# Two-level Strassen for left and right from block 2 on, and all second-level weight pieces in iteration 0

## Chip, cores and metric

The kernel runs on one core of a Trainium2 chip. The metric is device time in microseconds for the whole program, from one launch; the kernel before takes 2949.6 us (median of three runs, 2948.95 to 2950.2). All data is fp32. A core has five engines: PE (matrix products), DVE, ACT and POOL (elementwise work), and SP, which here only issues DMAs. ACT and POOL issue some DMAs too. Each engine takes its instructions in one order.

## What is computed

Two graph layers on 128 graphs of 64 nodes with 768 features. Only layer 0's products with W_left and W_right, and what lies around them in time, are touched by the change.

```python
# layer 0, per graph (h = x, 64 x 768; adjacency 64 x 64)
p = softmax(h @ h.T / sqrt(768)); delta = p * adjacency
attn = delta / (delta.sum(-1, keepdims=True) + 1e-10)
h_left, h_self, h_right = (h @ W.T + b for W, b in left, self, right)
ctx = upper(attn) @ h_left + diag(attn)[:, None] * h_self + lower(attn) @ h_right
x1 = layernorm(h + relu(layernorm(ctx) * gamma + beta))
# layer 1, 12 heads of 64
q, k, v = x1 @ Wq + bq, x1 @ Wk + bk, x1 @ Wv + bv
scores = where(adj > 0, q @ k.T / 8 + beta * adj, -9e15)
out = layernorm(x1 + concat_heads(softmax(scores) @ v))
```

## The kernel before

**Blocks and stages.** The 8192 rows are worked on as 16 blocks of 512 rows (8 graphs). A block needs six 512 x 768 x 768 products: left, right, self (layer 0), q, k and v (layer 1). Each is done by Strassen's algorithm, which replaces eight products of half-size matrices by seven: `seven` (L354) runs over `ORDER`, the seven products i, and over two halves j. That makes 14 *places*, numbered 0 to 13, each of three products on PE (recorded as six instructions, two passes each). A Strassen sum of activations is formed on POOL (`combined` L301, `combined4` L315), a Strassen piece of a weight was formed once at the program's start and is streamed from HBM by SP.

**Iteration n of the main loop** works on layer 0 of block m = n + 1 and layer 1 of block n, in this order: left and right of block m (`left` and `right`), self (`own`), v of block n (`val`, in which the context products of block m stand too, `context0` L647), then q and k in three groups of heads hg 0, 1, 2 (`qk[0]` to `qk[2]`, `projected` L776). Iteration 0 has only `val` and `qk`; block 1's layer 0 is done before the loop. The dictionaries in brackets are *hooks*: a function put at a place of such a stage is called in front of that place's products.

**One level and two.** For m below `DEEP` (3), left and right are two calls of `side_part` (L585), each a `seven`. From block 3 on they are one call of `both_sides` (L603): `nested` (L409) does Strassen's algorithm twice, 7 x 7 = 49 products of left and right side by side, in the outer order `ORDER2`. Its 49 steps are counted as 28 places, those of left (0 to 13) and then those of right (14 to 27). The sums of the second level are formed on POOL by `second_level` (L320), into a tile with two buffers (`s2_p`); the nine pieces of a weight product are loaded by SP as tiles `wlr` from `lr_d` (L617), 63 loads for a block.

**Where the second-level weight pieces come from.** `deepened(i)` (L243) has three parts. `begin` loads the four half-pieces of product i into tiles `w_deep` (4 DMAs on SP) and copies the plain parts in HBM (4 DMAs on POOL, L254 and L255); two calls of `formed` (L257, L260) do four subtractions each on DVE; `end` (L262, L266) stores four results with POOL's DMAs. The tiles come from the pool `wst`, 19 buffers that all streamed weights (`wl`, `wr`, `ws`, `wv`, `wqk`, `wlr`) share. The three parts after `begin` are put at the head of the queue `urgent` three places later.

**The order of the work around the products.** No scheduler moves the instructions of the loop: on each engine they stand in the order in which the Python code issues them. What DVE and ACT do beside the products (softmax, norms, transposes) is put with `later` (L121) in one of three queues, `first`, `urgent` and `lazy`. After each place, `step` (L135) takes at most one full DVE item from them, with an ACT item before it where one is at the head. `settle(key)` (L157) takes items until none of that key is left: whatever needs a result settles it first. In `nested`, `step` takes no lazy item at three of the seven products.

**Names that matter below.** `attention0` (L498) needs block m's transposed rows `hT` (`turned` L289, six DVE transposes at L294), computes `u` (L516) and queues its softmax. `scores` (L804) computes `sc` (L822) for one group of heads and queues its softmax (L826, L847 to L849 on DVE, 16 ACT exponentials L840, two DVE transposes L844); `weighted` (L853) multiplies the result with v (L869) and adds it on DVE (L875, L879). `uqk` (L791) is ACT's read of a q or k product, `q`, `k` (L799) DVE's. `finish_by_act` (L884) is the last layernorm of block p = n - 1: four row sums on ACT (L921), a scaling on DVE (L896), four sums of squares on ACT (L924), DVE (L899), a root on ACT, DVE (L905, L906), four ACT normalisations (L910) and the stores (L914). `stored` (L705) settles layer 0's result of block n and stores it to HBM as `x1d`; `squares` (L278) then loads it as `sq` by four DMAs on ACT's queue (L285), in rows of short pieces, for the transposes of layer 1. In iteration 1 `stored` is at place 1 of `right` and the four `sq` loads are at places 2 to 5 of `right`; in later iterations they are at place 4 and at places 10 to 13 of `left`.

Of the kernel before, what the change touches and what calls it, by code (L numbers as in the profile page):

```python
# [13 lines left out]
ALU = mybir.AluOpType  # L14
# [4 lines left out]
B, L, D = 128, 64, 768  # L19
# [3 lines left out]
HALF = D // 2  # L23
# [21 lines left out]

ORDER2 = (7, 1, 2, 6, 5, 4, 3)
MATRICES = (1, 2, 8, 3, 9, 5, 7, 4, 6)
DEEP = 3


@with_exitstack
def gnn_two_layers(ctx: ExitStack, tc, x, adj, wl, bl, ws, bs, wr, br, gamma, beta,
                   wq, bq, wk, bk, wv, bv, abeta, out):
    nc = tc.nc
# [35 lines left out]
    bias_lr = const.tile([P, 2, D], F32, tag="bias_lr", name="bias_lr")  # L90
# [66 lines left out]
    def settle(key):  # L157

        for queue in (first, urgent, lazy):
            while any(item[0] == key or item[0][0] == key for item in queue):  # L160
                queue.popleft()[1]()
# [81 lines left out]
    def deepened(i):  # L243


        w = {}

        def begin():
            for j, nm in enumerate("lr"):
                src = pieces[nm][i]  # L250
                for k in range(2):
                    w[j, k] = wst.tile([P, 2, QUAD], F32, tag="w", name="w_deep")
                    nc.sync.dma_start(out=w[j, k], in_=src[:, k, :].rearrange("p (h c) -> p h c", h=2))
                nc.gpsimd.dma_start(out=lr_d[i - 1, 0:3, :, j, :].rearrange("m p c -> p m c"), in_=src[:, :, 0:QUAD])  # L254
                nc.gpsimd.dma_start(out=lr_d[i - 1, 3:5, :, j, :].rearrange("m p c -> p m c"), in_=src[:, 1:3, QUAD:HALF])  # L255

        def formed(j):  # L257
            b11, b12, b21, b22 = (w[j, k][:, h, :] for k in range(2) for h in range(2))
            for out, a, b in ((b11, b12, b11), (b12, b22, b12), (b22, b22, b11), (b21, b21, b22)):
                nc.vector.tensor_tensor(out, a, b, ALU.subtract)  # L260

        def end():  # L262
            for j in range(2):
                for k in range(2):
                    d = lr_d[i - 1, 5 + 2 * k : 7 + 2 * k, :, j, :].rearrange("m p c -> p m c")
                    nc.gpsimd.dma_start(out=d, in_=w[j, k])  # L266

        return begin, [(partial(formed, 0),), (partial(formed, 1),), (end, "gap")]
# [9 lines left out]
    def squares(rows):  # L278


        sq = sq_p.tile([P, SQ, Q * KC], F32, tag="sq", name="sq")
        by_group = rows.rearrange("(s j) (a f) -> a j s f", j=Q, a=P // Q)

        def load(a):
            nc.scalar.dma_start(out=sq[a * Q : (a + 1) * Q], in_=by_group[a])  # L285

        return sq, [partial(load, a) for a in range(P // Q)]
# [13 lines left out]
    def combined(xT, n=None):  # L301
# [6 lines left out]
        S = {1: a11, 2: a12, 4: a22, 5: s1, 6: s2, 7: a21}  # L308
        if n is not None and n >= DEEP:

# [696 lines left out]
    for n in range(NBLK):  # L1007
        m, p = n + 1, n - 1
        left, right, own, val = {}, {}, {}, {}
        qk = [{}, {}, {}]  # L1010

        def at(hooks, place, f, *args):
            hooks.setdefault(place, []).append(partial(f, *args))

        def spread(hooks, place, fs):
            for k, f in enumerate(fs):
                at(hooks, place + k, f)


        for i, (when, hooks, place) in zip(ORDER2, ((0, val, 2), (0, val, 8), (0, qk[0], 8), (0, qk[1], 6),  # L1020
                                                    (0, qk[2], 6), (1, own, 3), (1, val, 3))):
            if when == n:
                begin, steps = deepened(i)
                at(hooks, place, begin)
                at(hooks, place + 3, lambda i=i, steps=steps: urgent.extendleft([(("d", i), *f) for f in reversed(steps)]))

        last = n == NBLK - 1
        if p >= 0:
            one = left if not last else qk[0]
            at(one, 2, scores, p, 2, *((1,) if last else (2, None, 4)))  # L1030
            at(one, 5, weighted, p, 1)
            if not last and m < DEEP:
                at(left, 13, weighted, p, 2)
                at(right, 0, finish_by_act, p)
            elif not last:
                at(right, 1, weighted, p, 2)
                at(right, 2, finish_by_act, p)
            else:
                at(qk[1], 5, weighted, p, 2)

        if not last:
            if n > 0:
                if m + 1 < NBLK:
                    at(left, 4, edges, m + 1)
                at(*((left, 11) if m < DEEP else (right, 13)), sides, m)
                sq1 = {}

                def begin1():
                    blocks[n]["sq1"], sq1["fs"] = squares(blocks[n]["x_d"])


                when, place = (left, 10) if n > 1 else (right, 2)
                at(when, place, begin1)
                fetch = {}

                def begin2():
                    fetch["fs"] = loads(m)

                at(right, 8, begin2)
                for t in range(T):  # L1060
                    at(right, 8 + t, lambda t=t: fetch["fs"][t]())
                for a in range(P // Q):
                    at(when, place + a, lambda a=a: sq1["fs"][a]())
                at(own, 0, settle, ("f", p))

                def turn1():
                    blocks[n]["xT"] = turned(("t1", n), blocks[n]["sq1"], f"xT_{n}")
                    later(("m", n), *mask(n), queue=urgent)

                at(own, 3, turn1)  # L1070

                def sums1():
                    settle(("t1", n))
                    blocks[n]["S"] = combined(blocks[n]["xT"])

                at(own, 11, sums1)
                at(val, 0, lambda: combined4(blocks[n]["S"]))
                at(left, 6, lambda: combined4(blocks[m]["S"]))
                at(*((left, 4) if n > 1 else (right, 1)), blocks[n]["stored"])
                if m + 1 < NBLK:  # L1080
                    sq = {}

                    def begin():
                        blocks[m + 1]["sq"], sq["fs"] = squares(x_b[m + 1])

                    at(own, 11, begin)
                    for a in range(P // Q):
                        at(own if a < 3 else val, 11 + a if a < 3 else 0, lambda a=a: sq["fs"][a]())
                if m == DEEP:
                    settle("d")  # L1090
                if m < DEEP:
                    side_part(m, "l", None, left)
                    side_part(m, "r", None, right)
                    at(own, 0, lambda: nc.vector.tensor_tensor(bias_lr[:, :, HALF:D], bias_lr[:, :, HALF:D],
                                                               bias_lr[:, :, 0:HALF], ALU.subtract))
                else:
                    for t, f in enumerate(both_sides(m, {**left, **{2 * len(ORDER) + k: f for k, f in right.items()}})):
                        at(own, 1 + t, f)
                self_part(m, None, own)
            tiles, normal = context0(m)  # L1100
            for t, f in enumerate(tiles):
                at(val, 1 + 2 * t, f)
            for hooks, place, f in ((val, 9, normal[0]), (val, 13, normal[1]), (qk[0], 1, normal[2])):
                at(hooks, place, f)
            if m + 1 < NBLK:

                def turn0():
                    blocks[m + 1]["hT"] = turned(("t", m + 1), blocks[m + 1]["sq"], f"hT_{m + 1}")

                at(val, 6, turn0)  # L1110

                def scores0():
                    settle(("t", m + 1))
                    attention0(m + 1, False)

                def sums0():
                    blocks[m + 1]["S"] = combined(blocks[m + 1]["hT"], m + 1)

                at(qk[0], 4, scores0)
                at(qk[2], 8, sums0)  # L1120

        if not last:
            values(n, val)
        else:
            transposed1(n)
            at(qk[0], 9, lambda: later(("m", n), *mask(n), queue=urgent))
            blocks[n]["S"] = combined(blocks[n]["xT"])
            combined4(blocks[n]["S"])
        at(qk[1], 2, scores, n, 0)
        at(qk[2], 2, scores, n, 1)  # L1130
        if not last:
            at(qk[2], 5, weighted, n, 0)
        for hg in range(NHG):
            projected(n, hg, qk[hg])
# [49 lines left out]
```

## Time and profile before

| | |
|---|---|
| median of the runs | 2949.6 us |
| the profiled execution | 2950.66 us, of which the span is 2949.0 |
| PE busy | 2881.7 us, 17578 matrix instructions |
| DVE, ACT, POOL busy | 1993.3, 1125.9, 731.1 us |
| iteration 0 (block 0's layer 1), 212.09 to 308.13 | 96.04 us |
| left and right of block 2, 308.13 to 370.54 | 62.41 us |
| left and right of block 3, 493.76 to 550.28 | 56.52 us |
| loads of `wlr` | 819, 192 KB each |

Times of rows are microseconds from the span's start. A row of the trace in order of time gives start, length, engine, line, operation, the tile written and read, and how many equal instructions were merged; in brackets stands the idle time of the engine before it and what ended it. "ACTq" and "SPq" are DMAs issued by those engines. A window row gives for a stretch its length, then each engine's busy time and count, the share of full clock that PE was granted, the share of time that the 16 DMA engines were busy, and GB/s. A PE instruction is shown with its pipeline's latency, so that lengths overlap: the distance of starts tells the rate.

### The profile page before, as it was taken

To read this page: it belongs to the slowest core of one execution; us is meant where nothing else is said; L and a number is where in the kernel's file an instruction comes from. 1 tells how busy PE (TensorE), PEld (TensorE's weight loads), DVE (VectorE), ACT (ScalarE), POOL (GpSimd) and SP (SyncE) were. 2 spreads that over 40 slices of the span, in tenths; PEclk is the share of its full clock that TensorE was granted. 3 is DMA by queue.
4 is the path that set the end of the run, shared out by engine and by line. 5 is a ranking of instruction groups with operands and counts; after the bars stand their busy time and mean duration, and the time that the engine had idled before them with its cause. 6 is when DMAs were issued, how large, how long until landed. Compare 5 with 4: busy or idle time off the path is not lost.

```text
span 2949.0 us, 49959 instructions
## 1 busy us (share of the span) xinstructions
PE 2881.7 (98%) x17578; PEld 1936.0 (66%) x17578; DVE 1993.3 (68%) x4034; ACT 1125.9 (38%) x2116; POOL 731.1 (25%) x881
## 2 busy tenths in 40 slices
PE   8899999999999999999999999999999999999997
PEld 5557667575675856658576575766757567585685
DVE  5857777676676766767667576676767667676556
ACT  0104324444343542434434344443434424354354
POOL 3133122305023040321404124050230513313110
PEclk9999999999999999999999999999999999999998
DMA  9678786949668495785957759486694966849442
GB/s 328 198 271 260 232 245 183 266 132 273 171 193 249 137 289 155 204 238 156 278 150 224 221 168 272 138 254 188 183 261 137 279 165 197 244 140 285 140 127 87
DMA packets 440150, 613.18 MB, mean 208 GB/s; under 512 B 53584, under 2 KB 416720, under 8 KB 439904
## 3 DMA queue, kind: packets, MB, share of 16 engines
q1 hardware_dynamic: 361808, 492.79, 55.5%
q10 hardware_dynamic: 60848, 44.05, 8.2%
q0 software_dynamic: 17248, 73.15, 6.8%
q8 instruction: 143, 2.34, 0.3%
q14 instruction: 103, 0.84, 0.1%
HBM read 539.43 MB, written 77.27 MB: 209 GB/s over the span
## 4 chain that ended last, share of the span: by engine, by line
PE 86%; issue 4%; ACT 3%; POOL 2%; DVE 2%; DMA 2%; POOLq 0%; SPq 0%; ACTq 0%; DVEq 0%
PE ps_X L373 33%; PE ps_Y L373 25%; PE ps_Y L626 11%; PE ps_X L626 10%; PE ps_ctx L665 3%; ACT eT L840 2%; PE sc L822 2%; PE ps_y L869 2%; PE u L516 1%; POOL q L326 1%; ACT L840 1%; DMA b_l<-in_L_gnn_W_left_dram 1%; ACT uqk L791 1%; POOL q L325 0%; POOL q L327 0%
## 5 line engine op out<-in xcount | busy, mean ns | idle before, releaser
L373 PE MATMUL ps_X<-xT,wqk 128*128 128x256 f32 x1728 | 395.9, 381 | 9.5 <-ACT uqk L791 9.5
L840 ACT ACTIVATE eT<-s 32x256 f32<-32x256 f32 x768 | 317.7, 414 | 177.5 <-DVE s L849 167.4
L373 PEld LDWEIGHTS ps_X<-xT,wqk 128*128 128x128 f32 x1728 | 326.1, 190 | 66.8 <-ACT uqk L791 16.2
L306 POOL TENSOR_TENSOR S<-hT 128x768 f32<-128x768 f32 x16 | 28.9, 1808 | 1139.9 <-PE ps_Y L373 1102.1
L373 PE MATMUL ps_Y<-S,wqk 128*128 128x256 f32 x1152 | 264.3, 379 | 0.0
L670 ACT ACTIVATE unused<-o 128x768 f32<-128x768 f32 x60 | 50.6, 844 | 499.8 <-DVE o L667 244.9
L373 PEld LDWEIGHTS ps_Y<-S,wqk 128*128 128x128 f32 x1152 | 219.1, 190 | 29.6
L427 DVE TENSOR_TENSOR lr<-ps_Y,u_deep 128x384 f32<-128x384 f32 x273 | 152.0, 557 | 108.1 <-PE ps_Y L626 82.4
L626 PE MATMUL ps_Y<-wlr,q 128*128 128x384 f32 x546 | 208.6, 491 | 0.0
L373 PE MATMUL ps_X<-wv,xT 128*128 128x384 f32 x576 | 195.0, 489 | 0.0
L791 ACT ACTIVATE uqk<-ps_X,bq 128x256 f32<-128x256 f32 x144 | 68.1, 473 | 325.1 <-PE ps_X L373 323.8
L373 PE MATMUL ps_X<-ws,hT 128*128 128x384 f32 x540 | 179.5, 487 | 3.0 <-DVE u L404 3.0
L799 DVE TENSOR_TENSOR q<-ps_Y,uqk 128x256 f32<-128x256 f32 x144 | 61.0, 423 | 177.7 <-ACT uqk L791 89.4
L879 DVE SCALAR_TENSOR_TENSOR o<-ps_y,rz,o 128x64 f32<-128x64 f32 x768 | 165.0, 277 | 6.8
L626 PE MATMUL ps_X<-wlr,q 128*128 128x384 f32 x364 | 151.2, 497 | 15.0 <-POOL q L326 6.0
L373 PEld LDWEIGHTS ps_X<-wv,xT 128*128 128x128 f32 x576 | 108.2, 190 | 80.8 <-issue 8.4
L427 DVE TENSOR_TENSOR u_deep<-ps_X,lr 128x384 f32<-128x384 f32 x195 | 107.3, 550 | 67.8 <-PE ps_X L626 66.2
L373 PEld LDWEIGHTS ps_X<-ws,hT 128*128 128x128 f32 x540 | 102.4, 190 | 75.0 <-DVE u L404 4.0
L626 PEld LDWEIGHTS ps_Y<-wlr,q 128*128 128x128 f32 x546 | 101.7, 190 | 67.1
L404 DVE TENSOR_TENSOR u<-ps_X,bv 128x384 f32<-128x384 f32 x96 | 53.4, 556 | 128.2 <-PE ps_X L373 128.2
L373 PE MATMUL ps_X<-S,wqk 128*128 128x256 f32 x576 | 138.2, 385 | 0.0
L373 PE MATMUL ps_Y<-xT,wqk 128*128 128x256 f32 x576 | 135.6, 385 | 0.0
(248 smaller groups left out, 5493.5 us busy)
## 6 DMA issues: line engine op xcount, KB each, us to landing
wlr<-lr_d SPq DMA_DIRECT2D x819, 192.0 KB, 3.4
wqk<-qk_d SPq DMA_DIRECT2D x672, 192.0 KB, 2.4
wv<-d_v SPq DMA_DIRECT2D x192, 192.0 KB, 2.9
ws<-d_s SPq DMA_DIRECT2D x180, 192.0 KB, 6.0
wv<-in_L_gnn_Wv_dram SPq DMA_DIRECT2D x144, 192.0 KB, 4.1
ws<-in_L_gnn_W_self_dram SPq DMA_DIRECT2D x135, 192.0 KB, 5.4
xa<-in_x_dram SPq DMA_DIRECT2D x64, 384.0 KB, 5.3
out_dram<-o POOLq DMA_DIRECT2D x64, 384.0 KB, 6.4
```

The lines of the kernel that those rows point to most:

```text
L373: nc.tensor.matmul(ps, lhsT=a, rhs=b, start=(c == 0 and i in (1, 2, 5)), stop=(c == len(fs) - 1), skip_group_check=True)
L404: nc.vector.tensor_tensor(u, ps, bias[nm][:, b * HALF : (b + 1) * HALF], ALU.add)
L427: nc.vector.tensor_tensor(dst, view(ps), add, ALU.add)
L626: nc.tensor.matmul(ps, lhsT=a, rhs=b, start=(k == 0 and j in (1, 2, 5)), stop=(k == len(fs) - 1), skip_group_check=True)
L665: nc.tensor.matmul(ps[g * L : (g + 1) * L, 0:HALF], lhsT=blk["aT"][:, t, g * L : (g + 1) * L], rhs=blk["lr"][t][:, g, cols], start=True, s ...
L670: nc.scalar.activation(unused(), o[t], AF.Identity, accum_out=total[:, t : t + 1])
L791: nc.scalar.activation(u, ps, AF.Identity, bias=bias["qk"[j]][:, c : c + 1])
L799: nc.vector.tensor_tensor(dst, ps, part, ALU.add)
L822: nc.tensor.matmul(sc[r][g * L : (g + 1) * L, t, c, :], lhsT=q[rows, c, tok], rhs=k[rows, c, tok], start=True, stop=True)
L840: nc.scalar.activation(e[cols, :, rows], pairs[rows, :, cols], AF.Exp)
L869: nc.tensor.matmul(y[r, h][cols, t, c, :], lhsT=eT[rows, 2 * h + t, c, cols], rhs=v[rows, 2 * h + t, g, hg + c * HC, :], start=True, stop= ...
L879: nc.vector.scalar_tensor_tensor(res[:, r, c, hg, :], ps[:, t, k, 0:HD], rz[:, t, k : k + 1], res[:, r, c, hg, :], ALU.mult, ALU.add)
```

## The change

`DEEP` goes from 3 to 2, so block 2's left and right are done by `both_sides`. All seven pieces of `deepened` are formed in iteration 0, at places 1, 5 and 9 of `val`, 2 and 8 of `qk[0]`, 2 and 8 of `qk[1]`; before, five were formed there (2 and 8 of `val`, 8 of `qk[0]`, 6 of `qk[1]`, 6 of `qk[2]`) and two in iteration 1 (place 3 of `own` and of `val`). The bias difference that two levels need is formed ahead of block 2's left and right instead of after them. By m < DEEP, iteration 1 also takes the other branch for three hooks: `weighted(p, 2)` moves from place 13 of `left` to place 1 of `right`, `finish_by_act(p)` from place 0 to place 2 of `right`, and `sides(m)` from place 11 of `left` to place 13 of `right`.

```diff
-DEEP = 3
+DEEP = 2
...
-        for i, (when, hooks, place) in zip(ORDER2, ((0, val, 2), (0, val, 8), (0, qk[0], 8), (0, qk[1], 6),
-                                                    (0, qk[2], 6), (1, own, 3), (1, val, 3))):
+        for i, (when, hooks, place) in zip(ORDER2, ((0, val, 1), (0, val, 5), (0, val, 9), (0, qk[0], 2),
+                                                    (0, qk[0], 8), (0, qk[1], 2), (0, qk[1], 8))):
...
                 if m == DEEP:
                     settle("d")
+                    nc.vector.tensor_tensor(bias_lr[:, :, HALF:D], bias_lr[:, :, HALF:D], bias_lr[:, :, 0:HALF],
+                                            ALU.subtract)
                 if m < DEEP:
                     side_part(m, "l", None, left)
                     side_part(m, "r", None, right)
-                    at(own, 0, lambda: nc.vector.tensor_tensor(bias_lr[:, :, HALF:D], bias_lr[:, :, HALF:D],
-                                                               bias_lr[:, :, 0:HALF], ALU.subtract))
```

## The prediction

> **What bounds the kernel now.** I read the page's engine line first: the span is TensorE's.
>
> ```profile
> span 2949.0 us, 49959 instructions
> ...
> PE 2881.7 (98%) x17578; PEld 1936.0 (66%) x17578; DVE 1993.3 (68%) x4034; ACT 1125.9 (38%) x2116; POOL 731.1 (25%) x881
> ```
>
> So an edit is worth what it does to PE's instruction count and to its few gaps. Busy time by stage comes next: block 0's layer 1 (212 to 308), block 2's left and right at one level, block 3's at two levels.
>
> ```profile
> core 0: us, PE busy (x) PEld busy (x) DVE busy (x) ACT busy (x) POOL busy (x), PEclk, DMA share, GB/s
> 212.09:308.13 96.04, 95.44 (x659) 70.96 (x658) 72.17 (x157) 40.44 (x80) 37.60 (x42) 1.00 0.73 236
> 308.13:370.54 62.41, 60.48 (x366) 36.12 (x364) 44.00 (x103) 17.59 (x39) 5.38 (x7) 0.97 0.78 229
> 493.76:550.28 56.52, 55.20 (x352) 32.20 (x350) 39.69 (x98) 21.67 (x42) 31.05 (x43) 1.00 0.98 284
> ```
>
> The first stage has 0.6 us of PE gap and DVE busy for three quarters of it; the last has DMA full. Then PE's order of time, where slack is read:
>
> ```profile
> 251.00 3.02 PE L516 MATMUL u<-hT 128*64 128x64 f32 x96
> ...
> 294.41 1.16 PE L869 MATMUL ps_y<-v,eT 64*64 64x65 f32 x64
> ...
> 337.21 0.70 PE L869 MATMUL ps_y<-v,eT 64*64 64x65 f32 x32 [0.75 <-DVE eT L844]
> 339.09 0.70 PE L869 MATMUL ps_y<-v,eT 64*64 64x65 f32 x32 [1.18 <-DVE eT L844]
> 339.72 3.86 PE L373 MATMUL ps_Y<-wl,S 128*128 128x384 f32 x6
> ```
>
> DVE and ACT give what those products wait for, and, last, how late block 2's and block 3's `finish_by_act` run:
>
> ```profile
> 250.23 1.09 DVE L294 STREAM_TRANSPOSE hT<-sq 128x512 f32<-128x512 f32 x1
> ...
> 276.06 1.22 DVE L849 TENSOR_TENSOR s<-s,mx 128x1024 f32<-128x1024 f32 x1
> 282.79 2.97 DVE L260 TENSOR_TENSOR w_deep<-w_deep 128x192 f32<-128x192 f32 x8
> 291.09 1.30 DVE L844 STREAM_TRANSPOSE eT<-eT 128x512 f32<-128x512 f32 x2
> ...
> 536.57 0.17 DVE L896 TENSOR_SCALAR f<-f 128x4 f32<-128x4 f32 x1
> ```
>
> ```profile
> 284.66 3.39 ACT L840 ACTIVATE eT<-s 32x256 f32<-32x256 f32 x8
> ...
> 360.25 0.93 ACT L924 ACTIVATE unused<-o,f 128x768 f32<-128x768 f32 x1 [6.95 <-DMA ws<-in_L_gnn_W_self_dram]
> ...
> 522.03 10.05 ACTq L285 DMA_DIRECT2D sq<-x1d  x3
> 532.19 0.84 ACT L921 ACTIVATE unused<-o 128x768 f32<-128x768 f32 x1 [10.44 <-DVE rz L875]
> ```
>
> The 6.95 us is ACT standing behind its own `sq` load, which waits for a weight load on SP.
>
> **What the skill says.** (1) The Trainium skill, PSUM — Partial Sum Buffer, section Engine vs sequencer instructions: ScalarE, VectorE and GpSimdE work strictly first in, first out. The 6.95 us above agrees. (2) TensorE: Matmul & The Clock Gate, What's actually happening: after an idle window of some 3.4 us PE falls to half clock, and a busy window restores it. Agrees: after the two waits at 336 to 339 six records of 0.32 us lasted until 343.37, that is 3.65 us instead of 1.94, 1.7 lost, and the granted clock of 340 to 344 was 0.57. (3) DMA: Bandwidth & Descriptors, Specifications: below 512 B a transfer loses rate. Agrees: ACT's queue, with the `sq` gathers, needed 8.2% of the span for 44.05 MB, SP's 55.5% for 492.79, so 1.65 times as long per byte.
>
> **The change, part by part.** Sums are against the profiled execution (2950.66 us, span 2949.0); its runs' median is 2949.6.
>
> *Block 2 at two levels.* 168 PE records (`wl`, `wr`) become 154 (`wlr`, 1/13 of the count for blocks 3 to 15): 14 x 0.3225 us (3.87 per 12) = 4.5. Evacuations on DVE, the sums on POOL and 63 loads on SP in place of 42 are all in block 3's stage, so the price of the whole is 56.52 - 62.41 = **-5.9**; the other 1.4 are the waits (1.93) and the half clock (1.7) of the old stage, less the small gaps of the new one. Bounds -7.5 and -4.5.
>
> *All seven `deepened` in iteration 0.* Each puts on DVE 8 subtractions (2.97), on SP 4 loads, on POOL 8 DMAs of about 0.72 (POOL is busy 38 of 96, so nothing). Two move here from iteration 1, where they cost PE nothing, and all stand earlier. In the built order 24 subtractions instead of 16 now precede the sixth `hT` transpose. Followed instruction by instruction: three transposes are left at 249.9; q, T4, k, T5, T6 end at 253.7, not 251.3. `attention0`'s products (251.0) need T6 by about 251.6: **+2.4** (1.8 to 3).
>
> In hg 1 the subtractions are at the head of the queue at places 5, 6, 11 and 12, so the first softmax (L847, L848, L849) is pushed to places 8 to 10, behind them and behind block 2's own softmax, which the late `u` and the swaps of v on ACT have put to places 2 to 4. With the shift of 2.4, DVE does s (L826) until 275.6, block 2's softmax until 279.6, eight subtractions until 282.6, one row of context until 283.6, q at 283.6, then L847, k, L848 and L849 at 1.22, 0.4, 1.21 and 1.22: the end is about 288 instead of 277.2. Its 16 exponentials all come after hg 2's first `uqk` (290.8 with the shift of 2.4): 16 x 0.425, one `uqk` of 0.4 between, end 298.1; the transpose ends 298.85; `weighted` wants it at 294.41 + 2.4 = 296.8. It is 2.1 late, and its second half waits for the next scores' two multiplications (0.64 each), 1.4 more: **+3.5** (2 to 4.5). The next scores are then late too: the wait for `uqk` at place 10 grows from 0.6 to 1.2, with the boundary **+0.7** (0 to 1.5).
>
> Weight loads share the 19 slots of `wst`. In the new order `wv` for i=4 waits for the first `deepened`'s stores (issued about 226 to 231, landing 3.6), with 2 to 3 us to spare; `wqk` for place 2 has about none. I take 0 (to 3).
>
> *Iteration 1, the hooks of left and right.* `stored` is at place 15 of block 2's stage (place 4 in block 3): it forces four L703 (0.65) and a reciprocal between evacuations, and POOL's sums stand behind four stores: **+1.5** (0 to 2.5).
>
> *The `sq` loads on ACT.* In block 3 they are at places 10 to 13 and `finish_by_act` at 16: counted from the stage's start, L921 begins at 38.4 and L896 at 42.8, just after the last load. In block 2 the loads stay at places 16 to 19, so that three of them stand ahead of L921 on ACT. The built program makes them wait: the first for x1d (stores at 34, landing 4.5: about 40), the second and third for the 58th and 62nd of 63 `wlr` loads, whose slots come free at about 36 and 41.5. Landing is 3.4 on the page, 6.8 in block 3's late stretch: third load at about 47.5. Four L921 (1.07 each) end at 52.1. L896 on DVE waits for them, and behind it stand the evacuations that PE's product at 45.3 + 1.5 needs: free at 53.5, **+6.7**. The fourth `sq` load waits for the third `xa` load (about 52.5), L924 x4 end at 57, L899 blocks DVE again: **+1.6**. Bounds of the pair 4 and 11.
>
> *Half clock* after such gaps: 1.7 at 340; three candidates, partly inside other waits: **+1.0** (0 to 4).
>
> *The `bias_lr` subtraction* (0.96) moves ahead of the stage; the next product to need DVE has 3 us: 0.
>
> Sum: -5.9 + 2.4 + 3.5 + 0.7 + 1.5 + 8.3 + 1.0 = +11.5: 2962.2 by the profiled execution, **2961** by the median.
>
> **Rivals.**
> *DVE has room and the loads land in time*, so the ACT chain holds nobody: for it, iteration 1's ACT wait of 6.95 us stopped no PE; against it, L896 stands directly before an evacuation. Gives 11.5 - 8.3 = +3.2, 2953.
> *All is covered (faster)*: the subtractions only fill DVE's idle quarter. It decides at two points: last `hT` transpose by 251.6, `eT` transpose by PE's arrival. Then only the stage counts: -5.9 to -7, 2943. Against: the queue is served in order, and the slack read there is 0.3 and 2.
> *The slots of `wst` bind*: SP, in order, stands at a `deepened` store while PE's own weights are behind it. For: in the first stage SP already waits 9.7 us for such stores ahead of `wqk` loads, DMA full from 236 to 260. Price: 3 us at two or three places, 2968 to 2971.
> *It does not do what it says*: no; the built program has 882 `wlr` loads for 819.
>
> **How the numbers follow.** Likeliest (in-order waits as worked out) 0.72, room on DVE 0.14, covered 0.04, slots 0.10. A measurement here tells 0.2% (5.9 us) from no change. The likeliest spans 2954 to 2968; with half of the room case and most of the slots case the range is 2953 to 2969. Faster 0.04; within 0.2% 0.14 (room, and the low edge of the likeliest, less its high edge); slower 0.82.
>
> **What would show it.** Right: `sq` loads on ACT at about 355 to 368 with L921 behind them, a PE wait of 5 or more us released by DVE behind L896 in block 2's stage; waits of 2 to 4 us at `u` (251) and at `ps_y` (297); from block 3 on the same 56.5. Wrong: block 2's stage near 57 us, or PE waits released by `wv` or `wqk` loads.

## The result and the profile after

The changed kernel takes **2967.76 us** (median of 4 runs, 2967.3 to 2968.69) against 2949.9 for the kernel before in the same comparison (4 runs, 2948.95 to 2951.79): a ratio of 1.0061, 95% interval 1.0049 to 1.0073. Slower by 0.6%. The forecast was 2961 in a range of 2953 to 2969, slower with a chance of 0.82. The profiled execution took 2968.69 us.

First the page of the changed kernel: its span and busy times.

```profile
span 2966.9 us, 50071 instructions
...
PE 2884.3 (97%) x17564; PEld 1934.6 (65%) x17564; DVE 1990.1 (67%) x4035; ACT 1135.4 (38%) x2130; POOL 758.4 (26%) x921
```

PE has 14 instructions fewer, as forecast, and yet 2.6 us more busy time: a sign of half clock. The three windows of the changed kernel that answer to those of before (iteration 0; block 2's left and right; block 3's), with length, busy time by engine and, behind POOL, the granted clock:

```profile
213.10:319.33 106.23, 99.63 (x659) 73.50 (x657) 76.59 (x169) 38.92 (x80) 49.09 (x62) 0.97 0.79 264
319.33:387.50 68.17, 58.13 (x351) 33.22 (x350) 44.16 (x109) 21.86 (x43) 31.11 (x43) 0.92 0.89 251
510.72:567.24 56.52, 55.19 (x351) 32.17 (x350) 39.71 (x98) 21.67 (x42) 31.07 (x43) 1.00 0.97 291
```

Iteration 0 grew from 96.04 to 106.23 (+10.2). Block 2's stage grew from 62.41 to 68.17 (+5.8) though it is now the kind of stage that takes 56.52 in block 3. These two make 16.0 of the 17.9 us by which the span grew. The rest lies outside them. v of iteration 0 starts 1.0 later; over the kernels below, which up to there are the same program but for early pieces in two, that start lies between 211.9 and 214.4 (222.3 in one of those two), so this is spread. And from the end of block 2's stage to the end of the program it is 2579.4 us against 2578.5, with 2577.7 to 2581.3 below, but for one that is told there. Part of this is hardly spread: from the start of block 15's left and right to the end it is 299.3 us against 297.6 before, and 299.1 to 300.0 in all kernels below but one (297.5, the kernel that begins two pieces earlier). In the changed kernel POOL stands idle for 2.96 us there, ahead of its last stores, and the profile names nothing that it waits for. POOL's DMAs stand in another order in these kernels than before; whether that is the cause was not tried.

PE's order of time in iteration 0, changed kernel; in brackets PE's idle time and what ended it:

```profile
252.02 1.53 PE L373 MATMUL ps_Y<-xT,wqk 128*128 128x256 f32 x6 [1.19 <-DMA wqk<-qk_d]
255.13 0.34 PE L516 MATMUL u<-hT 128*64 128x64 f32 x4 [0.96 <-DVE hT L294]
256.10 2.44 PE L516 MATMUL u<-hT 128*64 128x64 f32 x76 [0.63 <-DVE hT L294]
284.51 5.42 PE L373 MATMUL ps_X<-xT,wqk 128*128 128x256 f32 x24 [1.19 <-DMA wqk<-qk_d]
302.42 0.70 PE L869 MATMUL ps_y<-v,eT 64*64 64x65 f32 x32 [2.13 <-DVE eT L844]
303.50 1.73 PE L869 MATMUL ps_y<-v,eT 64*64 64x65 f32 x32 [0.38 <-DVE s L826]
305.15 2.93 PE L373 MATMUL ps_X<-S,wqk 128*128 128x256 f32 x6
307.87 3.85 PE L373 MATMUL ps_Y<-S,wqk 128*128 128x256 f32 x12
```

DVE of the changed kernel, ahead of `u` and ahead of hg 1's softmax:

```profile
253.66 0.42 DVE L799 TENSOR_TENSOR k<-ps_Y,uqk 128x256 f32<-128x256 f32 x1 [1.32 <-PE ps_Y L373]
254.00 2.04 DVE L294 STREAM_TRANSPOSE hT<-sq 128x512 f32<-128x512 f32 x2
...
286.59 0.42 DVE L799 TENSOR_TENSOR q<-ps_Y,uqk 128x256 f32<-128x256 f32 x1 [1.71 <-ACT uqk L791]
```

PE's waits at `u` (1.59) and at `ps_y` (2.51) are where the forecast put them, and two waits for `wqk` loads (2.38) are where it put none. DVE was not at work all the way to its late instructions: it stood idle for 1.32 in front of `k` and for 1.71 in front of `q`. The last two rows of PE are slow: from start to start six instructions took 2.72 us and twelve 3.69, where the kernel with both cures below needs 1.40 and 2.59 for the same rows. Half clock thus cost 2.4 there and up to 0.8 more in the row of `ps_y`.

In block 2's stage, three views of the changed kernel: PE, ACT and DVE.

```profile
373.40 1.65 PE L626 MATMUL ps_X<-wlr,q 128*128 128x384 f32 x2 [8.17 <-DVE u_deep L427]
374.83 1.49 PE L626 MATMUL ps_X<-wlr,S 128*128 128x384 f32 x2
376.11 2.56 PE L626 MATMUL ps_Y<-wlr,S 128*128 128x384 f32 x4
```

```profile
360.02 8.26 ACTq L285 DMA_DIRECT2D sq<-x1d  x3
368.38 0.84 ACT L921 ACTIVATE unused<-o 128x768 f32<-128x768 f32 x1 [19.55 <-DMA wlr<-lr_d]
```

```profile
372.25 0.17 DVE L896 TENSOR_SCALAR f<-f 128x4 f32<-128x4 f32 x1 [9.66 <-ACT unused L921]
...
380.21 0.17 DVE L899 TENSOR_SCALAR f<-f 128x4 f32<-128x4 f32 x1 [3.92 <-ACT unused L924]
```

Read them from the bottom. DVE stood 9.66 us at a scaling of 0.17 us because ACT had not finished L921; ACT stood at three DMA issues, the last of which went when a `wlr` load had landed; and PE stood 8.17 us behind an evacuation queued after L896. Then eight instructions took 1.43 + 1.28 + 2.40 us from start to start, not 0.72 + 0.65 + 1.29: 2.45 more. The second such wait, at L899, stopped DVE for 3.92 but PE not at all: PE was late itself by then.

### The profile page after: what moved, and what is told of

Same layout as the page of the kernel before. It is cut to its first block, busy times and chain, and to the rows that moved or that the text cites. A ratio compares the mean times of both kernels' runs of the same rounds, so it can differ in the third digit from the quotient of the medians.

```text
span 2966.9 us, 50071 instructions
## 1 busy us (share of the span) xinstructions
PE 2884.3 (97%) x17564; PEld 1934.6 (65%) x17564; DVE 1990.1 (67%) x4035; ACT 1135.4 (38%) x2130; POOL 758.4 (26%) x921
## 4 chain that ended last, share of the span: by engine, by line
PE 85%; issue 4%; ACT 3%; DMA 3%; DVE 2%; POOL 2%; SPq 0%; ACTq 0%; POOLq 0%; DVEq 0%
PE ps_X L373 31%; PE ps_Y L373 23%; PE ps_Y L626 12%; PE ps_X L626 11%; PE ps_ctx L665 3%; ACT eT L840 2%; PE ps_y L869 2%; PE sc L822 2%; PE u L516 1%; POOL q L326 1%; ACT L840 1%; DMA b_l<-in_L_gnn_W_left_dram 1%; ACT uqk L791 1%; DMA wlr<-lr_d 0%; POOL q L325 0%
## 5 line engine op out<-in xcount | busy, mean ns | idle before, releaser
L427 DVE TENSOR_TENSOR lr<-ps_Y,u_deep 128x384 f32<-128x384 f32 x294 | 163.7, 557 | 113.0 <-PE ps_Y L626 86.1
L626 PE MATMUL ps_Y<-wlr,q 128*128 128x384 f32 x588 | 224.6, 491 | 0.0
L626 PE MATMUL ps_X<-wlr,q 128*128 128x384 f32 x392 | 163.6, 499 | 24.2 <-DVE u_deep L427 8.2
L427 DVE TENSOR_TENSOR u_deep<-ps_X,lr 128x384 f32<-128x384 f32 x210 | 115.5, 550 | 72.3 <-PE ps_X L626 70.5
L626 PEld LDWEIGHTS ps_Y<-wlr,q 128*128 128x128 f32 x588 | 109.4, 190 | 72.4 <-DVE lr L427 0.3
L306 POOL TENSOR_TENSOR S<-xT 128x768 f32<-128x768 f32 x16 | 28.9, 1808 | 422.9 <-DVE xT L294 301.0
```

The costliest lines, as they stand in the source:

```text
L306: nc.gpsimd.tensor_tensor(s1, a21, a22, ALU.add)
L427: nc.vector.tensor_tensor(dst, view(ps), add, ALU.add)
L626: nc.tensor.matmul(ps, lhsT=a, rhs=b, start=(k == 0 and j in (1, 2, 5)), stop=(k == len(fs) - 1), skip_group_check=True)
```

## The experiments

Twelve kernels. Under each stand iteration 0 and block 2's left and right in its profiled execution, and its time. Each ratio is to runs of the kernel before on the same chip (medians 2950.4 to 2951.2 there).

**Block 2's stage: the `sq` loads.** In the first kernel they stand six places later, in the second where later blocks have them, with `stored`.

```diff
-                when, place = (left, 10) if n > 1 else (right, 2)
+                when, place = (left, 10) if n > 1 else (right, 8)
```

> The changed kernel with iteration 1's four `sq` loads six places later (right 8 for right 2), so that all four stand behind L921 and L924 on ACT instead of three ahead of L921. Theory (ACT in order: L921 stands behind three loads that wait for weight loads, DVE's L896 behind L921, PE behind DVE): PE's wait of 8.17 us behind L896 and the half clock after it (about 2.5) go; block 2's left and right 57 to 58.5 us instead of 68.2; total 2956.5 to 2959. Rival (L896 is late for another reason: DVE's own queue, or the full DMA, is late in this stage and the loads only lie in the same place): stage 64 or more, total 2963 or more. Iteration 0 is as in the changed kernel, 106 us, under both.

Measured: 2962.59 us, ratio 1.0042 (1.0027 to 1.0057). Iteration 0 103.8, the stage 62.96: between the two theories, for a reason that the profile shows. Two of the loads fell between L924 and the root L902, and the second of them, waiting for a `ws` load, held that root. ACT, DVE and PE of this kernel:

```profile
370.76 0.32 ACTq L285 DMA_DIRECT2D sq<-x1d  x1
371.12 0.20 ACT L902 ACTIVATE f<-f 128x4 f32<-128x4 f32 x1 [6.34 <-DMA ws<-in_L_gnn_W_self_dram]
```

```profile
371.36 0.18 DVE L905 RECIPROCAL f<-f 128x4 f32<-128x4 f32 x1 [4.20 <-ACT f L902]
```

```profile
372.77 1.62 PE L626 MATMUL ps_X<-wlr,q 128*128 128x384 f32 x2 [3.13 <-issue]
```

L921 was no longer held, the wait of 8.17 was gone, and the same chain stood a link further on with 3.13. The profile names no releaser for this wait; DVE's evacuation `u_deep` behind L905 ended at 372.67, just before it. So the chain moves with the loads: what brings their waiting to PE is their place in ACT's queue, not a backlog of DVE.

```diff
-                when, place = (left, 10) if n > 1 else (right, 2)
+                when, place = (left, 10)
...
-                at(*((left, 4) if n > 1 else (right, 1)), blocks[n]["stored"])
+                at(left, 4, blocks[n]["stored"])
```

> The changed kernel with iteration 1's `stored` (place 15 to 4) and its `sq` loads (places 16 to 19 to 10 to 13) where all later blocks have them. Theory: the same gain as with the loads put later, and what `stored` at place 15 cost on top (forecast: 1.5): stage 56.5 to 57.5, total 2955 to 2958. Rival (DVE enters the stage late from iteration 0, and an earlier `stored` forces x1's steps into a queue that is still behind): a new PE wait in places 4 to 8, stage 60 or more, total 2960 or more.

Measured: 2956.62 us, ratio 1.0018 (1.0011 to 1.0025); iteration 0 103.3, the stage 57.72, no wait behind L896, L899 or L905. This is the stage that the theory asked for but for 0.2 us (PE waited 1.40 for POOL's sums), and the time is 11 us under the changed kernel's. Iteration 0 still has its 7.2 us over the kernel before. (Its profiled execution also lost 6.6 us at one set of `ws` loads in iteration 4, which no other kernel shows.)

**Iteration 0: the pieces.** The kernel before with nothing but the seven new places (of the lines on places, here and below, only the list is shown):

```diff
 DEEP = 3
...
-((0, val, 2), (0, val, 8), (0, qk[0], 8), (0, qk[1], 6), (0, qk[2], 6), (1, own, 3), (1, val, 3))
+((0, val, 1), (0, val, 5), (0, val, 9), (0, qk[0], 2), (0, qk[0], 8), (0, qk[1], 2), (0, qk[1], 8))
```

> The kernel before (block 2 at one level) with only the seven places of the changed kernel: all seven `deepened` in iteration 0. Theory (the lateness of iteration 0 is the order of DVE's queue and of the weight slots, and needs nothing of block 2's second level): iteration 0 at 106 us as in the changed kernel (96 before), block 2's stage at its old 62.4 or a little under, total 2959 to 2961.5. Rival (the sums of block 2's second level on POOL, or the chain of loads for it, make iteration 0 late): iteration 0 at 97 to 100, total 2950 to 2954.

Measured: 2966.61 us, ratio 1.0053 (1.0038 to 1.0068). Iteration 0 104.2, with the same waits at `u` (0.96 and 0.63) and `ps_y` (2.14); block 2's old stage 64.7, with its old waits before `ps_y` and a new one of 1.97 at its end. So iteration 0 is late by 8.1 of the 10.2 us with the places alone; it does not need the second level of block 2. The total is 5 over the theory's range: the stage came out 2.3 longer and not a little shorter, the end of the program 1.7 longer, and the profiled execution is 2.8 faster than the median.

```diff
-((0, val, 1), (0, val, 5), (0, val, 9), (0, qk[0], 2), (0, qk[0], 8), (0, qk[1], 2), (0, qk[1], 8))
+((0, val, 2), (0, val, 8), (0, qk[0], 5), (0, qk[0], 9), (0, qk[1], 6), (0, qk[2], 6), (0, qk[2], 9))
```

> The changed kernel with the seven `deepened` at other places of iteration 0: v 2 and 8, hg 0 5 and 9, hg 1 6, hg 2 6 and 9; so 16 subtractions stand ahead of the `hT` transposes, and hg 1 has one piece instead of two ahead of its softmax. Theory (what binds is which pieces stand ahead of the `hT` and `eT` transposes on DVE and of the `wqk` loads on SP): iteration 0 at 97 to 101 us, block 2's stage unchanged at about 68 or up to 2 longer, total 2959 to 2964. Rival (the volume of seven pieces in 96 us binds, wherever they stand): iteration 0 at 104 or more, total 2965 to 2972.

Measured: 2964.79 us, 0.8 over the range, ratio 1.0049 (1.0034 to 1.0064). Iteration 0 fell to 95.56, under that of the kernel before, so seven pieces as such are no bound. But the stage rose to 75.87: the last two pieces' subtractions stand at its head, PE waits 2.21 for an evacuation behind them and 2.18 for `wlr` loads, and the ACT chain of 8.28 is still there. The cost had only crossed the boundary.

The same places with `stored` and `sq` as in later blocks:

> The spread places of the `deepened` (v 2, 8; hg 0 5, 9; hg 1 6; hg 2 6, 9) together with `stored` and the `sq` loads of iteration 1 at the places of later blocks. Theory (the two parts are separate: the chain of loads on ACT belongs to block 2's stage, and what the late pieces cost moves over the boundary): iteration 0 at 95.5 to 97 us as with the spread alone, block 2's stage 64 to 66 (75.9 with the spread alone, less the wait of 8.3 and its half clock of 2.5), total 2952 to 2956. Rival (the late pieces also delay x1's steps, so that the earlier `stored` waits for them): stage 68 or more, total 2957 or more.

Measured: 2957.3 us, ratio 1.0024 (1.0017 to 1.0031); iteration 0 95.53, the stage 65.69. Both stages are as forecast from separate parts, the median 1 us over its range. In the stage this is in part chance: the waits for `wlr` shrank to 0.30, and a new wait of 3.35 came behind DVE.

**DVE's time, or something else?** The next kernel has the 56 subtractions on POOL, the changed kernel's places, and the later blocks' `stored` and `sq`.

```diff
-                nc.vector.tensor_tensor(out, a, b, ALU.subtract)
+                nc.gpsimd.tensor_tensor(out, a, b, ALU.subtract)
```

> The seven pieces at the changed kernel's own places, `stored` and `sq` of iteration 1 as in later blocks, and the 56 subtractions of `deepened` on POOL instead of DVE. Estimate from POOL's rows: 128x128 costs 0.53 us, 128x384 1.00, so 128x192 about 0.65; 36 us more on POOL in iteration 0, where it is busy 49 of 106. Theory (what binds in iteration 0 is DVE's queue: the subtractions ahead of the `hT` and `eT` transposes): the waits at `u` (1.6) and at `ps_y` (2.5) go, iteration 0 at 96 to 99, block 2's stage 56.5 to 58, total 2944 to 2949. Rival (slots and order of the weight loads bind, or the sums on POOL come late behind the subtractions): waits released by `wqk`, `wv` or POOL, iteration 0 at 102 or more, total 2951 or more.

Measured: 2981.16 us, ratio 1.0101 (1.0087 to 1.0115), the slowest of all; iteration 0 129.5 (103.3 with the same `stored` and `sq` and the subtractions on DVE), the stage 57.68. DVE's busy time in iteration 0 fell to 60.4 us, yet the waits at `u` (1.30 and 0.63) and `ps_y` (2.14 and 0.20) were still there. A subtraction took 0.65 on POOL as estimated, but they stand among POOL's Strassen sums, keep their `wst` buffers longer, and PE waited up to 5.00 for `wqk`. This is what the rival of the slots looks like when it is real.

Then the changed kernel with three of four subtractions left out:

```diff
-for out, a, b in ((b11, b12, b11), (b12, b22, b12), (b22, b22, b11), (b21, b21, b22)):
+for out, a, b in ((b11, b12, b11),):
```

> The changed kernel with three of the four subtractions of every `formed` left out (14 of 56 remain; the pieces that are stored are then partly the undiminished ones). All loads, stores, slots and places stay. Theory (DVE's queue binds in iteration 0): no wait at `u`, none of the 2.1 at `ps_y`, iteration 0 at 96 to 99; block 2's stage as in the changed kernel, 66 to 69; total 2957 to 2961. Rival (the loads, stores and slots of the pieces bind): the waits for `wqk` stay or grow and iteration 0 takes 102 or more, total 2963 or more.

Measured: 2967.39 us, ratio 1.0050 (1.0035 to 1.0066); iteration 0 106.28, the same as with all 56. **Neither theory holds**: the numbers are the rival's, but the waits are still 0.96 and 0.63 at `u`, 2.13 and 0.38 at `ps_y`, and those are no loads. (That the sum is the same to 0.05 us is partly chance: the `wqk` loads cost one wait of 2.25 with 1.7 of half clock behind it, in place of two of 1.19.) DVE of this kernel shows why:

```profile
252.91 0.38 DVE L799 TENSOR_TENSOR k<-ps_Y,uqk 128x256 f32<-128x256 f32 x1
253.21 2.03 DVE L294 STREAM_TRANSPOSE hT<-sq 128x512 f32<-128x512 f32 x2
...
287.26 0.42 DVE L799 TENSOR_TENSOR q<-ps_Y,uqk 128x256 f32<-128x256 f32 x1 [5.54 <-ACT uqk L791]
287.61 1.21 DVE L847 TENSOR_TENSOR s<-s,add 128x1024 f32<-128x1024 f32 x1
```

The last two `hT` transposes stand behind `k`, which reads the very product that PE finishes before it asks for `u`; shorter subtractions do not bring them forward. The softmax L847 had its input by 276, and stood behind a `q` for which DVE sat idle 5.54 us. The first wait at `ps_y` is 2.13 or 2.14 in all six kernels with these places and two turns for `formed`, whether DVE does all subtractions, a quarter or none, and whether `wqk` is late by 0.4 us or by over 10. This suggests that a piece does not push the transposes and the softmax back by its time, but by the **turns** that it takes: `step` gives one DVE item per place, and each piece takes two turns of the queue `urgent`, in which they stand, for its `formed` and one for `end`. The next kernel tests that.

**The turns alone.** Both `formed` in one item, all 56 subtractions kept:

```diff
-        return begin, [(partial(formed, 0),), (partial(formed, 1),), (end, "gap")]
+        return begin, [(lambda: (formed(0), formed(1)),), (end, "gap")]
```

> The changed kernel with both `formed` of a `deepened` in one step of the queue instead of two: the same 56 subtractions, loads, stores and begins, but each piece takes one turn less in the hand-made order. In the built order all `hT` transposes then stand ahead of hg 0's first `q` (two of them stand behind `k` in the changed kernel), and the first softmax one pair of products earlier. Theory (turns, not DVE time: a piece pushes `hT` and the softmax behind evacuations that wait for PE's own products): no wait at `u`, none or under 0.5 of the 2.5 at `ps_y`, iteration 0 at 97 to 100 us though DVE does all 56 subtractions; block 2's stage at 66 to 69; total 2957 to 2962. Rival (the forecast's reason: DVE's time, 24 subtractions ahead of the last transpose): the wait at `u` stays at 1.6 or more, iteration 0 at 103 or more, total 2964 or more.

Measured: 2961.89 us, ratio 1.0039 (1.0025 to 1.0052); iteration 0 100.86, 0.9 over the theory's range, the stage 66.55. The waits at `u` and `ps_y` and those for `wqk` are gone, while DVE was busier in iteration 0 (79.7 us) than in the changed kernel. DVE of this kernel:

```profile
245.98 2.97 DVE L260 TENSOR_TENSOR w_deep<-w_deep 128x192 f32<-128x192 f32 x8
...
249.40 1.09 DVE L294 STREAM_TRANSPOSE hT<-sq 128x512 f32<-128x512 f32 x1
...
250.47 1.08 DVE L294 STREAM_TRANSPOSE hT<-sq 128x512 f32<-128x512 f32 x1
251.46 0.39 DVE L799 TENSOR_TENSOR q<-ps_Y,uqk 128x256 f32<-128x256 f32 x1
```

The last transpose ends at 251.55 and `q` follows it, with 24 subtractions in v before it. What stays of iteration 0's excess (4.8) is now DVE's time: 0.80 behind eight subtractions in v, 1.84 behind eight more before hg 1's scores, and 1.6 of half clock after the second. In the stage the `sq` loads stopped DVE at L896 for 4.29 and at L899 for 6.99, and PE waited twice, 2.81 and 3.49 (for the second the profile names no releaser; DVE's evacuation behind L899 ended 0.1 before it did). Where the first wait is short, the second reaches PE.

Both cures together, and two variants of it:

> Both cures together: `formed` in one step, and `stored` and `sq` of iteration 1 at the places of later blocks. Theory (turns in iteration 0, the chain of loads on ACT in block 2's stage, nothing else): iteration 0 at 97 to 100, stage 56.5 to 58, total 2945 to 2950, no slower than the kernel before. Rival (something else of the seven pieces, the weight slots above all, costs 4 or more even so): waits for `wqk` of 2 or more with half clock, total 2952 or more.

Measured: **2950.56 us, ratio 1.0003 (0.9995 to 1.0011)**. Both stages are in the theory's ranges, iteration 0 with 99.25 and the stage with 56.53; the median is 0.6 over its. Windows of this kernel:

```profile
212.54:311.79 99.25, 96.04 (x658) 70.92 (x657) 79.62 (x176) 41.46 (x83) 49.87 (x62) 1.00 0.83 283
311.79:368.32 56.53, 55.20 (x351) 32.17 (x350) 42.19 (x101) 21.67 (x42) 30.85 (x43) 1.00 0.98 287
```

The 17.9 us of the change are gone, with two edits of order. The next kernel, with both cures too, moves one piece ahead of iteration 0 and spreads the others:

```diff
+    begin7, steps7 = deepened(ORDER2[0])
+    pre[12] = [begin7]
+    side_part(1, "r", None, pre)
...
+            at(val, 0, lambda: urgent.extendleft([(("d", ORDER2[0]), *f) for f in reversed(steps7)]))
...
+((0, val, 2), (0, val, 8), (0, qk[0], 5), (0, qk[0], 9), (0, qk[1], 6), (0, qk[2], 3))
```

> As the kernel with both cures, but one piece begins ahead of iteration 0 (place 12 of block 1's `right`, its subtractions at place 0 of v) and the other six at v 2 and 8, hg 0 5 and 9, hg 1 6, hg 2 3. Theory: six pieces in iteration 0, none at its end, iteration 0 at 96 to 97.5 and the stage at 56.5 to 57.5, total 2944 to 2948 unless the loads ahead of iteration 0 make `right` late (DMA full until 190 there). Rival (that lateness, as with two pieces ahead: 2 to 4 us before v): v starts at 215 or later, total 2949 or more.

Measured: 2952.36 us, ratio 1.0006 (0.9998 to 1.0014); iteration 0 97.16 as asked for, the stage 59.49 and the total over their ranges, though v started at 214.2. Again a saving before the boundary came back behind it, as waits of 1.04 for an evacuation and 0.49 for `wlr`. An earlier try moved two pieces ahead (places 9 and 12), with `formed` still in two items and the other five as in the kernel before:

> Two of the seven pieces begin in the last stage ahead of iteration 0 (places 9 and 12 of block 1's `right` product, subtractions at 12 and at place 0 of v), the other five where the kernel before has its first five; `stored` and `sq` of iteration 1 as in later blocks. Theory (DVE has room before iteration 0, being busy 6.4 of 15 us there, and five pieces in iteration 0 cost nothing as in the kernel before): iteration 0 at 96 to 98, the part before it up to 1 us longer, block 2's stage 56.5 to 58, total 2943 to 2948. Rival (DMA is full until 190 there and the slots bind): the start of v later than 214, or iteration 0 at 100 or more, total 2950 or more.

Measured: 2956.82 us, ratio 1.0020 (1.0011 to 1.0028); iteration 0 96.21 and the stage 58.74, about as asked for, but the total is over its range, since v started at 222.3: PE waited 2.32 for an evacuation behind subtractions whose `w_deep` loads came late (DVE idle 7.68 for them), while some 5 us were lost in the first 31 us of the span, ahead of anything that differs. How much of its time is the pieces' stays open.

Last, the kernel with both cures and its two remaining DVE waits attacked:

```diff
-((0, val, 1), (0, val, 5), (0, val, 9), (0, qk[0], 2), (0, qk[0], 8), (0, qk[1], 2), (0, qk[1], 8))
+((0, val, 1), (0, val, 4), (0, val, 9), (0, qk[0], 2), (0, qk[0], 8), (0, qk[1], 2), (0, qk[1], 6))
```

> The kernel with both cures, its second piece at v 4 for 5 and its last at hg 1 6 for 8. There PE still waits 0.80 us behind the second piece's eight subtractions (at 241) and 1.59 us behind the last piece's (before hg 1's scores at 293). Theory (these two are DVE's time: 2.97 us of subtractions in one go, put where DVE has just been idle or where no product of PE follows at once): both waits go or fall under 0.5, iteration 0 at 96.2 to 97.5, stage unchanged at 56.5, total 2946 to 2949, the fastest of all. Rival (DVE's backlog in hg 1 only shifts, to `q` at 284 or to the softmax and `ps_y` at 298; or w_deep's loads one place earlier delay `wv`): a new wait of 1.5 or more, iteration 0 at 99 or more, total 2950 to 2953.

Measured: 2949.75 us, ratio 0.9999 (0.9991 to 1.0007). Iteration 0 98.18, 0.7 over its range, the stage 56.52. The wait in v is gone, that before the scores is 0.61, and 0.74 came back as waits for `wqk`. It beats the changed kernel and ties with the kernel before and with both cures: "the fastest of all" is not shown. By its two stages it should be 3.8 us faster than the kernel before (5.9 won by the second level, 2.1 lost in iteration 0), which the interval does not reach; less the 1.7 at the end of the program it is 2.1, and that is below what these runs can tell.

## Why the forecast was right, and where it was not

The direction, the range and the two places were right. Of its signs of being right, the wait behind L896 came as described and the wait at `u` was shorter than the 2 us named; of its signs of being wrong, one came: PE waits released by `wqk` loads. By the steps of the forecast:

- **Block 2 at two levels, -5.9**: right. Freed of the chain the stage took 56.53 and 56.52, against 62.41.
- **`u`, +2.4**: the place was right, the wait 1.59. The order that the forecast followed (`q`, a transpose, `k`, two transposes) is the order of the trace. **The reason failed**: it counted the time of 24 subtractions in place of 16 ahead of the sixth transpose. With a quarter of them the wait stayed, with all of them in fewer turns it went. It is the turn behind `k`, worth the two transposes themselves.
- **`ps_y`, +3.5**: 2.51 of waiting. That ACT's exponentials stand behind hg 2's `uqk`, and the softmax behind a `q`, was right; that DVE works off subtractions up to that `q` was not: it stood idle in front of it, for 1.71 in the changed kernel and for 5.54 with a quarter of them.
- **Next scores and boundary, +0.7**: nothing; the old wait of 0.6 before the last `q` products went.
- **Weight loads, 0 (to 3)**: 2.38 in two waits. The forecast saw that `wqk` had about nothing to spare and took 0 all the same. The waits were gone when each piece took one turn less, and far greater with the subtractions on POOL, which fits buffers held until `end` has its turn; but more buffers by themselves were not tried, so this cause is not shown.
- **`stored`, +1.5**: at most 0.5 (a wait of 0.66 for POOL's sums, 0.21 without it).
- **The `sq` loads on ACT, +6.7 and +1.6**: 8.17 and 0. Loads, L921, L896, evacuation, PE: each link as forecast. The second link, at L899, is real too: it cost PE 3.49 in the kernel with the turns alone, and nothing here, where PE was late already. The Trainium skill's section Engine vs sequencer instructions (PSUM — Partial Sum Buffer) calls ACT's and DVE's queues strictly first in, first out; both waits, 8.17 here and 3.13 with the loads put later, agree.
- **Half clock, +1.0 (0 to 4)**: the term most mis-sized. About 3.2 in iteration 0 (2.4 in two rows and some 0.8 in the row before them) and 2.45 in the stage, 5.6 in all. That is 4.6 of the 6.4 us by which the sum fell short; `wqk` is 2.4 more, and L896 1.5 more, while `u`, `ps_y`, L899, `stored` and the scores gave 5.7 back. The start and the end of the program add 1.9. The rest is for the most part what the waits cost beyond their listed idle time (2.0 at `u` by the distance of starts, for 1.59 listed). That the range held is thus in part luck: terms that were too small by 8.5 us were made up for by others that were too large.

The rival of "room on DVE" had a point that the forecast missed: DVE did have room in iteration 0. Given even more of it (42 subtractions fewer), it sat idle in front of the instruction that held up the softmax, and PE waited as before.

## What to carry to other kernels

Where a hand-made order gives one item per product, a moved step costs turns and not only microseconds, and here mostly turns: count which evacuations it pushes its followers behind, and ask on which product of PE those wait. Test "this engine is too busy" by taking its time away and leaving the order, and then the order by leaving the time; here the two gave opposite answers. And a DMA issued from a compute engine's queue belongs behind that engine's urgent work only if nothing urgent comes after it either: moved six places, one of the same four loads stopped a later instruction of ACT instead.

## What was not expected of the hardware

The Trainium skill (TensorE: Matmul & The Clock Gate, What's actually happening) says that PE falls to half clock after an idle window of about 3.4 us and that this window runs freely, not from the kernel's own start. The second half fits: at the same place, ahead of block 2's second product, a wait of 2.21 was followed by slow instructions in the kernel with spread places, and one of 2.20 by none in the kernel with spread places and later blocks' `sq`. The first half is not the limit here: waits of 1.84, 1.97 and 2.13 us (the last with one of 0.38 soon after it) were followed by 1.6 to 3.2 us of lost rate, while waits of 1.59 and 1.95 were not. The case at 340 us that the forecast called an agreement was none for this half either: its two waits were 0.75 and 1.18 us. So in these runs a wait of about 2 us on PE cost either nothing more or about as much again, and its length did not tell which. A sum of waits must carry that.
